# Two cross-product layers on one core: whole first loads, one weight transfer, one sum moved to VectorE and a few copies moved on ScalarE

## The chip, the cores and the metric

The kernel runs on one core of a Trainium2 chip. The metric is the device time of one execution in microseconds. The kernel before took 2045.71 us (median of four runs, 2044.89 to 2046.76). Five engines matter: TensorE (PE; its weight loads are shown apart as PEld), VectorE (DVE), ScalarE (ACT), GpSimd (POOL) and SyncE (SP), which issues most of the DMAs.

## The reference

The input `r_x` has 4096 rows, 32 fields and 16 values per field. Everything runs in float32. A layer multiplies every channel of its input with every field of `x`, mixes the products with a weight matrix and normalises over rows and values:

```python
def _cin_layer(out, x, W, b, gamma, beta):
    r, _, e = x.shape
    h = jnp.einsum('rne,rfe->rnfe', out, x).reshape(r, -1, e)
    h = jnp.einsum('rce,oc->roe', h, W) + b[None, :, None]
    return _batchnorm(h, gamma, beta)
h1 = _cin_layer(x, x, W1, b1, g1, beta1)
out, direct1 = (h1[:, :64], h1[:, 64:])
direct2 = _cin_layer(out, x, W2, b2, g2, beta2)
agg = jnp.concatenate([direct1, direct2], axis=1)
return agg.sum(axis=-1)
```

The batch norm needs the mean and the variance over all rows before the second layer can begin, so the kernel has two stages with a short passage between them.

## The kernel before, in words

The 65536 sites (rows times values) are cut into 128 tiles of T = 512 sites.

**Stage one** walks over the tiles t = 0 to 127. As x times x is symmetric, each tile needs 512 + 16 products and not 1024. `load_main(t)` fetches two tiles, `a` and `b` (128 partitions by 1024 floats, 512 KB each, on SP's queue). VectorE multiplies them into `z` (line 387, 128x2048), and four matmuls with `w1_sb[:, 0..3]` add it up in a bank `ps` (line 428). The 16 products that are left of each tile are computed for eight tiles at once in `zr` (line 373, from `r`), and four small matmuls with `w1_sb[:, 4..5]` add them for four tiles (line 380). ScalarE then evicts the bank three times (lines 352, 355, 358), VectorE takes the statistics (line 115) and a sum (line 364). Tiles rotate through pools: `lpool` has 4 buffers, `zpool` 4, `psum` 6 banks. The weights are the sum of two halves of W1: ScalarE's queue loads `w1_sb` (line 308) and `w1m_sb` (line 309), 384 KB each, and POOL adds them in four pieces (line 312).

The beginning is special. Three matmuls of ones (line 239, "begun") occupy TensorE while the first data are on the way. Tile 0's `a` and `b` are loaded in halves of 256 KB (line 294), in the order a, b, b, a, and the products of tiles 0 and 1 are made in 128x512 pieces (line 396). For tiles 0 and 1 the leftovers come last on TensorE, after the eight matmuls. In this part of the program a scheduler sets the order of each engine's instructions from its own model of time; an edit can therefore move instructions that it doesn't touch.

**The passage**: the last four tiles are computed in halves so that the kept 64 channels come first (line 461). Their statistics give the scale `keep`, and the direct channels are multiplied while the second stage's first products are being made.

**Stage two** walks over 64 pairs of tiles c and, in each, over four stages k (the groups i of 16 kept channels, in the order 3, 0, 1, 2). It uses a Strassen-like scheme with seven products in place of eight. The order in which it issues its work is written out by hand: `queue` chains each engine's instructions. Per stage (c, k):

- ScalarE makes two factors, `f1` and `f2`, by normalising the kept channels into PSUM (line 659, `f<-a,keep`; two buffers, shared with `b11`, ScalarE's PSUM copy of one block of `zz`).
- VectorE multiplies them with `b` and `bx` into `zz` (line 667, two of 128x2048 per stage; stage (0, 0) in four pieces, line 672).
- T2 has two halves. `sum_first` lets POOL make the first (line 703, 128x512), `sum_rest` lets VectorE make the second (line 662, `t<-zz,b`), and POOL then makes T1 and T4 (line 714, 128x2048; in the first stages in two pieces of 128x1024). Stage (0, 0) needs no T.
- TensorE (line 698) runs x2, then the previous stage's `x54` (which needs T1 and T4), then `x31`, then `x67`, 28 passes in all. A pair's sums lie in four banks: X2 and X1, X6 and X2, X3 and X4, X5 and X7. With six banks for two pairs, the next pair's X3/X4 bank is the one that held X1; its first writer is `x31` in stage k = 0.
- `combine(c - 1)` runs in steps (`next(steps)`) among the stages of pair c. Its first step is three ScalarE copies out of the X1 bank (`both`, `both`, `e`); it comes in stage k = 0 after `f1` of the next stage has been queued. VectorE adds (`both`, `u`, `e`, `e`) and a reduction (line 833) follow. In k = 3 of the first seven pairs VectorE takes one more piece of postponed work from `idle` (line 641, statistics; line 364; line 137).

Of the kernel before, what the change touches and what calls it, by code (L numbers as in the profile page):

```python
# [41 lines left out]
FP = mybir.dt.float32  # L42
AF = mybir.ActivationFunctionType
ALU = mybir.AluOpType
AX = mybir.AxisListType

P = 128
ROWS, FIELDS, EMB = 4096, 32, 16
SITES = ROWS * EMB
HALF = SITES // 2  # L50
T = 512
# [5 lines left out]
WRAP = 48  # L57
# [10 lines left out]


@with_exitstack  # L70
def tile_cin(ctx: ExitStack, tc: tile.TileContext, xa, xb, xr, w1, w1m, w2, bn, out):
    nc = tc.nc

    const = ctx.enter_context(tc.tile_pool(name="const", bufs=1))
# [10 lines left out]
    def load_bn():  # L85
        bn_sb = const.tile([P, 6], FP, tag="bn", name="bn_sb")
        nc.scalar.dma_start(bn_sb, bn)
        return bn_sb
# [6 lines left out]
    class Stats:  # L95
# [15 lines left out]
        def add(self, h):  # L111

            if self.at == 0:
                self.stats = spool.tile([P, SG, 6], FP, tag=f"stats{self.name}", name=f"stats{self.name}")
            nc.vector.bn_stats(self.stats[:, self.at, :], h)  # L115
            self.at += 1
            if self.at == self.sizes[self.group]:
                group = self.groups[:, self.group]
                nc.vector.bn_aggr(group[:, 1:3], self.stats[:, : self.at].rearrange("p a b -> p (a b)"))
                nc.vector.tensor_scalar(group[:, 2:3], group[:, 2:3], float(self.at * T), None, ALU.mult)  # L120
                self.at = 0
                self.group += 1
# [83 lines left out]
    for g in range(NC // DIFF):  # L206
        at = 14 + 24 * g
# [7 lines left out]
    loads = []  # L215
# [12 lines left out]
    def queue(engine, make):  # L228

        with tc.issue_after(lasts[engine].ins) if engine in lasts else nullcontext():  # L230
            lasts[engine] = make()
        return lasts[engine]
# [5 lines left out]
    for _ in range(BEGIN):  # L238
# [7 lines left out]
        out=select,  # L246
# [16 lines left out]
    with ExitStack() as one:  # L263
# [5 lines left out]
        zpool = one.enter_context(tc.tile_pool(name="zpool", bufs=4))  # L269
# [5 lines left out]
        def load_rem(g):  # L275

            r = rpool.tile([P, 2 * T], FP, tag="r", name="r")
            with tc.issue_after(loads[-1].ins) if loads else nullcontext():
                nc.sync.dma_start(r, bass.AP(xr.tensor, xr.offset + g * P * 2 * T, [[2 * T, P], [1, 2 * T]]))
            return r  # L280

        def load_main(t):
            a = lpool.tile([P, 2 * T], FP, tag="a", name="a")
            b = lpool.tile([P, 2 * T], FP, tag="b", name="b")

            def load(to, part, n):
                at = part * T
                if to is a:
                    at += xa.offset + t * FIELDS * 2 * T
                    source = bass.AP(xa.tensor, at, [[2 * T, FIELDS], [0, 4], [1, n * T]])  # L290
                else:
                    at += xb.offset + (t * WRAP + 2) * T
                    source = bass.AP(xb.tensor, at, [[T, FIELDS], [4 * T, 4], [1, n * T]])
                return nc.sync.dma_start(to[:, part * T : (part + n) * T], source)

            if t == 0:

                parts = ((a, 0, 1), (b, 0, 1), (b, 1, 1), (a, 1, 1))
            else:
                parts = ((a, 0, 2), (b, 0, 2))  # L300
            for part in parts:
                last = load(*part)
            loads.append(last)
            return a, b

        w1_sb = wpool.tile([P, 6, P], FP, tag="w1", name="w1_sb")
        w1m_sb = zpool.tile([P, 6, P], FP, tag="z", name="w1m_sb")
        nc.scalar.dma_start(w1_sb, w1)
        nc.scalar.dma_start(w1m_sb, w1m)

        for k in (slice(0, 1), slice(1, 2), slice(2, 4), slice(4, 6)):
            nc.gpsimd.tensor_tensor(w1_sb[:, k], w1_sb[:, k], w1m_sb[:, k], ALU.add)  # L312
        bn_sb = load_bn()
        w2_sb = const.tile([P, 16, P], FP, tag="w2", name="w2_sb")
        s_sb = const.tile([P, 4, 4, 2, KEEP], FP, tag="s", name="s_sb")
        neg_sb = const.tile([P, 2, 2, KEEP], FP, tag="neg", name="neg_sb")
# [80 lines left out]

        ending = NT - ENDING
        main = [load_main(t) for t in range(FIRST)]
        r = load_rem(0)  # L400
        for t in range(NT - ENDING):
            s = t % GROUP
# [6 lines left out]
            z = zpool.tile([P, 2, 2, T], FP, tag="z", name="z")  # L409
# [84 lines left out]
        for c in range(NC - ENDING // 2, NC):  # L494
# [3 lines left out]
            for half, k in enumerate(ks):  # L498
                at = half_of[half]
                to = h[:, half * T : (half + 1) * T]  # L500
# [28 lines left out]
        for c in range(NC - ENDING // 2, NC):  # L529
# [10 lines left out]
            for half, k in enumerate(ks):  # L540
                at = half_of[1 - half]
                bias = (b1, b1_swapped)[half][at]
                to = eds[c][half_of[half]]
# [120 lines left out]
    def multiply(z, a, b):  # L664

        a = a.unsqueeze(1).unsqueeze(1).to_broadcast([P, 2, 2, T])
        dve(lambda: nc.vector.tensor_tensor(z, a, b.rearrange("p (k q) t -> p k q t", k=2), ALU.mult))  # L667

    def multiply_part(z, a, b, q):

        a = a.unsqueeze(1).to_broadcast([P, 2, T])
        dve(lambda: nc.vector.tensor_tensor(z[:, :, q], a, b.rearrange("p (k q) t -> p k q t", k=2)[:, :, q], ALU.mult))

    def factor(a, i, half):
        f = factors.tile([P, T], FP, tag="f", name="f")
        act(f, a[:, half * T : (half + 1) * T], scale=keep[:, i, 0:1], bias=keep[:, i, 1:2])
        return f
# [19 lines left out]
            self.started.add(x)  # L697
            queue("pe", lambda: nc.tensor.matmul(self.of[x], w, b, start=start, stop=stop))  # L698

    def sum_first(z):  # L700

        t2 = tpool.tile([P, 2, T], FP, tag="t2", name="t2")
        queue("pool", lambda: nc.gpsimd.tensor_tensor(t2[:, 0], z[:, 1, 0], z[:, 0, 0], ALU.add))  # L703
        return t2

    def sum_rest(z, b11, t2, by_q, by_k):

        t14 = upool.tile([P, 2, 2, T], FP, tag="t14", name="t14")
        add(t2[:, 1], z[:, 1, 1], b11)
        twice = t2.unsqueeze(1).to_broadcast([P, 2, 2, T])  # L710
        parts = (slice(0, 1), slice(1, 2)), (slice(0, 2),)
        for k in parts[not by_k]:
            for q in parts[not by_q]:
                queue("pool", lambda: nc.gpsimd.tensor_tensor(t14[:, k, q], z[:, 2 + k.start : 2 + k.stop, q], twice[:, k, q], ALU.subtract))  # L714
        return t2, t14
# [132 lines left out]
    steps, steps_before = iter(()), iter(())  # L848
# [7 lines left out]
    for c in range(NC):  # L856
        raw, b, bx = following
        sums_ = Sums()

        for k, i in enumerate(STAGES):  # L860

            z = z2pool.tile([P, 4, 2, T], FP, tag="zz", name="zz")
            t = None
            if c == k == 0:

                for q in range(2):
                    multiply_part(z[:, 0::3], f1, b, q)
                    multiply_part(z[:, 1:3], f2, bx, q)
            else:
                multiply(z[:, 0::3], f1, b)  # L870
                if k == 1:

                    next(steps, None)
                f2 = factor(raw[i], i, 1)
                b11 = factors.tile([P, T], FP, tag="f", name="b11")
                act(b11, z[:, 0, 1])
                if k == 1:

                    next(steps, None)
                multiply(z[:, 1:3], f2, bx)  # L880
                t2 = sum_first(z)

            next(steps_before if k == 0 else steps, None)
            if k == 3 and idle:
                dve(idle.pop(0))
            if c > 0 or k > 0:
                t = sum_rest(z, b11, t2, (c, k) <= (1, 0), (c, k) == (NC - 1, 3))
            if k < 3:
                f1 = factor(raw[STAGES[k + 1]], STAGES[k + 1], 0)
            elif c + 1 < NC:  # L890
                following = loaded(c + 1)
                f1 = factor(following[0][STAGES[0]], STAGES[0], 0)

            next(steps, None)
            for _ in range(min(len(sums_left), 4 if c == NC - 1 else 1)):
                queue("act", sums_left.pop(0))
            stage = Stage(sums_, i, z, t, k == 3)
            if c == k == 0:
                stage.ordinary()
            elif (c, k) == (NC - 1, 3):  # L900
                stage.at_last(waiting)
            else:
                stage.x2()
                if waiting:
                    waiting.x54()
                stage.x31()
                stage.x67()
            if c > 0 or k > 0:
                waiting = stage

            if c == 9 and k == 2:
                queue("act", direct_factors)
            if 10 <= c < 14 and k == 2:
                queue("act", lambda: scale_direct(c - 10))
            if c == 15 and k == 2:
                with tc.issue_after(loads[-1].ins):
                    write_direct()
        steps, steps_before = combine(c, sums_), steps
# [12 lines left out]
    part = ROWS // 8  # L931
# [77 lines left out]
```

## Time and profile before

| | |
|---|---|
| four runs | 2046.76, 2044.89, 2046.28, 2045.14 us (median 2045.71) |
| the profiled execution | 2046.76 us, its span 2045.0 us |
| stage one | from 8.85 us (first matmul on data) to about 480 |
| passage | about 480 to 492 us |
| stage two | 492 to 2028 us on TensorE |
| tail after TensorE's last matmul | about 17 us of the span |
| busy share | PE 99%, DVE 96%, POOL 73%, ACT 58% |
| one 128x512 pass of a matmul | 0.43 us apart in stage one, half of that on the mean in stage two (two halves of the array run side by side) |
| first seven transfers to land | w1 3.8, a 5.5, w1m 6.5, b 7.4, the second halves 8.0 and 8.6, tile 1's a 9.9 us |

All times within the execution are counted from the start of its span. A line of the timeline gives the start, the duration, the engine, the source line, the operation, what it writes and reads, the shapes, and in brackets how long the engine was idle before it and what ended that. "SPq" and "ACTq" are the issues of DMAs on these queues. A line of the view by stretches gives the stretch, its length, the busy time of each engine with its number of instructions, then the granted TensorE clock as a share of full speed, the share of the DMA engines' time and the rate. In the table of waits the columns are the total, the count and the longest.

### The profile page before, as it was taken

The numbers are of one execution on the slowest core, as the hardware profiler recorded it, in microseconds if no ns is written. First come the engines' busy times: TensorE is split into PE (matmuls) and PEld (weight loads), VectorE is DVE, ScalarE is ACT, GpSimd is POOL, SyncE is SP. The second block draws the span as 40 slices with busy tenths as digits, with TensorE's granted clock in tenths as the row PEclk, the third lists the DMA queues.
The fourth block names the chain that finished last, engine by engine and source line by source line (L and its number), as shares of the span: only waits on it lengthen the run. The fifth ranks groups of instructions, "written<-read, shape, count | busy, mean of one in ns | idle before, by whom it ended". The sixth has DMA issues, their size and how long they took to land.

```text
span 2045.0 us, 24467 instructions
## 1 busy us (share of the span) xinstructions
PE 2028.2 (99%) x8500; PEld 870.6 (43%) x8500; DVE 1960.7 (96%) x1521; ACT 1185.6 (58%) x1914; POOL 1483.8 (73%) x525
## 2 busy tenths in 40 slices
PE   9999999999999999999999999999999999999997
PEld 3444444443344444444444444444444444444443
DVE  8998988988999999999999999999999999999997
ACT  4555555554566666565666555656665565566564
POOL 0000000002999999999999999999999999999996
PEclk9999999999999999999999999999999999999999
DMA  9999999996777777777776767777767677777661
GB/s 391 371 345 366 352 364 370 371 357 191 177 177 179 178 174 173 196 173 184 180 175 166 175 171 179 176 178 182 175 165 175 172 174 184 179 177 175 167 163 42
DMA packets 112380, 440.70 MB, mean 215 GB/s; under 512 B 13056, under 2 KB 13056, under 8 KB 103808
## 3 DMA queue, kind: packets, MB, share of 16 engines
q1 hardware_dynamic: 105840, 418.43, 73.0%
q10 hardware_dynamic: 6416, 20.72, 2.6%
q8 instruction: 66, 1.08, 0.2%
q14 instruction: 58, 0.48, 0.1%
HBM read 417.07 MB, written 22.02 MB: 215 GB/s over the span
## 4 chain that ended last, share of the span: by engine, by line
PE 98%; DVE 1%; issue 0%; POOL 0%; DMA 0%; ACT 0%; DVEq 0%; ACTq 0%; POOLq 0%
PE x L698 74%; PE ps L428 21%; PE ps L380 2%; PE ps L461 1%; DMA w1m_sb<-in_w1m 0%; POOL t L714 0%; DVE zz L667 0%; DVE d L934 0%; POOL w_sb L312 0%; ACT u L659 0%; DVE both L662 0%; ACT both L659 0%; POOL t L703 0%; DVE d L833 0%; DVE t L662 0%
## 5 line engine op out<-in xcount | busy, mean ns | idle before, releaser
L714 POOL TENSOR_TENSOR t<-zz,t 128x2048 f32<-128x2048 f32 (+1 forms) x260 | 1161.7, 4469 | 20.7 <-DVE t L662 0.9
L698 PE MATMUL x<-t,s_sb 128*64 128x512 f32 x2040 | 958.3, 592 | 0.4 <-POOL t L714 0.4
L698 PE MATMUL x<-zz,s_sb 128*64 128x512 f32 x2048 | 933.7, 592 | 0.0
L698 PE MATMUL x<-zz,w_sb 128*64 128x512 f32 x2056 | 759.1, 592 | 0.0
L703 POOL TENSOR_TENSOR t<-zz 128x512 f32<-128x512 f32 x255 | 326.5, 1280 | 521.0 <-DVE zz L667 520.4
L667 DVE TENSOR_TENSOR zz<-f,bx 128x2048 f32<-128x2048 f32 x255 | 582.2, 2283 | 19.4 <-ACT f L659 19.4
L659 ACT ACTIVATE f<-a,keep 128x512 f32<-128x512 f32 x512 | 398.2, 778 | 342.8 <-DVE zz L667 296.4
L667 DVE TENSOR_TENSOR zz<-f,b 128x2048 f32<-128x2048 f32 x255 | 582.4, 2284 | 0.1
L698 PEld LDWEIGHTS x<-t,s_sb 128*64 128x64 f32 x2040 | 279.2, 137 | 495.5 <-issue 467.2
L698 PE MATMUL x<-t,w_sb 128*64 128x512 f32 x1020 | 479.3, 592 | 0.0
L428 PE MATMUL ps<-z,w_sb 128*128 128x512 f32 x992 | 435.9, 597 | 2.3 <-POOL w_sb L312 2.3
L698 PEld LDWEIGHTS x<-zz,s_sb 128*64 128x64 f32 x2048 | 279.5, 137 | 251.7 <-issue 244.9
L387 DVE TENSOR_TENSOR z<-a,b 128x2048 f32<-128x2048 f32 (+1 forms) x127 | 288.5, 2273 | 42.0 <-PE ps L428 33.1
L428 PEld LDWEIGHTS ps<-z,w_sb 128*128 128x128 f32 x992 | 186.4, 190 | 250.0 <-issue 237.5
L698 PEld LDWEIGHTS x<-zz,w_sb 128*64 128x64 f32 x2056 | 236.7, 137 | 123.6 <-issue 121.5
L659 ACT ACTIVATE b<-zz 128x512 f32<-128x512 f32 x255 | 152.3, 597 | 187.3 <-DVE zz L667 187.3
L352 ACT ACTIVATE e<-ps,bn_sb 128x512 f32<-128x512 f32 x124 | 85.2, 687 | 221.1 <-PE ps L428 201.3
L662 DVE TENSOR_TENSOR t<-zz,b 128x512 f32<-128x512 f32 x255 | 173.3, 680 | 0.4
L698 PEld LDWEIGHTS x<-t,w_sb 128*64 128x64 f32 x1020 | 139.6, 137 | 0.0
L596 ACT ACTIVATE unread<-e,center 128x512 bf16<-128x512 f32 x122 | 86.2, 706 | 0.0
L358 ACT ACTIVATE ed<-ps,bn_sb 64x512 f32<-64x512 f32 x124 | 84.8, 684 | 2.3
L115 DVE BATCH_NORM_STATS2 stats<-e 128x6 f32<-128x512 f32 x124 | 85.1, 687 | 1.1 <-ACT e L352 1.1
(103 smaller groups left out, 866.4 us busy)
## 6 DMA issues: line engine op xcount, KB each, us to landing
a<-h SPq DMA_DIRECT2D x256, 512.0 KB, 4.5
b<-in_xb SPq DMA_DIRECT2D x64, 1024.0 KB, 8.4
a<-in_xa SPq DMA_DIRECT2D x127, 512.0 KB, 6.6
b<-in_xb SPq DMA_DIRECT2D x127, 512.0 KB, 7.7
bx<-in_xb SPq DMA_DIRECT2D x64, 512.0 KB, 8.4
bx<-x SPq DMA_DIRECT2D x64, 512.0 KB, 10.2
h<-kept ACTq DMA_DIRECT2D x64, 256.0 KB, 5.6
r<-in_xr SPq DMA_DIRECT2D x16, 512.0 KB, 9.0
```

The lines of the kernel that those rows point to most:

```text
L115: nc.vector.bn_stats(self.stats[:, self.at, :], h)
L352: nc.scalar.activation(e, ps, AF.Identity, bias=b1)
L358: done = nc.scalar.activation(ed[to, :], ps[KEEP:, :], AF.Identity, bias=b1[KEEP:])
L387: return nc.vector.tensor_tensor(z[:, k], a.rearrange("p (a t) -> p a t", a=2)[:, k].unsqueeze(2).to_broadcast([P, n, 2, T]), b.rearrange( ...
L428: nc.tensor.matmul(pss[t], w1_sb[:, m, :], z[:, m // 2, m % 2, :], start=t < FIRST and m == 0, stop=t >= FIRST and m == 3,)
L596: return nc.scalar.activation(unread, e[:, s], AF.Square, bias=center[:, s], accum_out=squares[:, s, c : c + 1])
L659: return queue("act", lambda: nc.scalar.activation(to, source, AF.Identity, **scale_bias))
L662: return dve(lambda: nc.vector.tensor_tensor(to, x, y, ALU.add))
L667: dve(lambda: nc.vector.tensor_tensor(z, a, b.rearrange("p (k q) t -> p k q t", k=2), ALU.mult))
L698: queue("pe", lambda: nc.tensor.matmul(self.of[x], w, b, start=start, stop=stop))
L703: queue("pool", lambda: nc.gpsimd.tensor_tensor(t2[:, 0], z[:, 1, 0], z[:, 0, 0], ALU.add))
L714: queue("pool", lambda: nc.gpsimd.tensor_tensor(t14[:, k, q], z[:, 2 + k.start : 2 + k.stop, q], twice[:, k, q], ALU.subtract))
```

## The change

There are three parts.

1. The beginning. Every `load_main` issues two whole loads of 512 KB, tile 0 included (four transfers of 256 KB before). The host packs the main weights (pieces 0 to 3) of both halves side by side: one transfer `w1_both` of 512 KB on ScalarE's queue, with 4 KB in each row, in place of two of 384 KB. VectorE adds them in one 128x512 instruction (line 298 of the changed kernel), placed ahead of the products. Pieces 4 and 5 of both halves (`left_both`, 256 KB) are loaded on SP's queue behind the loads of tiles 0 and 1 and ahead of `r`, and POOL adds them (128x256).
2. In stage (0, 1) of stage two, VectorE makes both halves of T2. POOL's line 703 is left out there.
3. In the pairs c = 1 to 4, the three copies out of the X1 bank are queued on ScalarE ahead of `f1` of stage (c, 1), and no longer behind it. (Pair 0 has no pair before it to combine.)

The order of the built program shows three more movements. SP issues two DMAs fewer ahead of tile 1's loads and one more (`left_both`) ahead of `r`. In stage one VectorE's order is changed over the first 20 tiles: the first `BNStats` stands ahead of tile 3's product, where it stood behind it, and later ones move by one or two places. TensorE's order is the same throughout.

```diff
@@ tile_cin: load_main and the weights
-            def load(to, part, n):
-                at = part * T
-                if to is a:
-                    at += xa.offset + t * FIELDS * 2 * T
-                    source = bass.AP(xa.tensor, at, [[2 * T, FIELDS], [0, 4], [1, n * T]])
-                else:
-                    at += xb.offset + (t * WRAP + 2) * T
-                    source = bass.AP(xb.tensor, at, [[T, FIELDS], [4 * T, 4], [1, n * T]])
-                return nc.sync.dma_start(to[:, part * T : (part + n) * T], source)
-
-            if t == 0:
-
-                parts = ((a, 0, 1), (b, 0, 1), (b, 1, 1), (a, 1, 1))
-            else:
-                parts = ((a, 0, 2), (b, 0, 2))
-            for part in parts:
-                last = load(*part)
-            loads.append(last)
+            nc.sync.dma_start(
+                a, bass.AP(xa.tensor, xa.offset + t * FIELDS * 2 * T, [[2 * T, FIELDS], [0, 4], [1, 2 * T]])
+            )
+            at_b = bass.AP(xb.tensor, xb.offset + (t * WRAP + 2) * T, [[T, FIELDS], [4 * T, 4], [1, 2 * T]])
+            loads.append(nc.sync.dma_start(b, at_b))
             return a, b
...
-        w1m_sb = zpool.tile([P, 6, P], FP, tag="z", name="w1m_sb")
-        nc.scalar.dma_start(w1_sb, w1)
-        nc.scalar.dma_start(w1m_sb, w1m)
-
-        for k in (slice(0, 1), slice(1, 2), slice(2, 4), slice(4, 6)):
-            nc.gpsimd.tensor_tensor(w1_sb[:, k], w1_sb[:, k], w1m_sb[:, k], ALU.add)
+        w1_both = zpool.tile([P, 2, 4, P], FP, tag="z", name="w1_both")
+        nc.scalar.dma_start(w1_both, w1)
         bn_sb = load_bn()
+        left_both = zpool.tile([P, 2, 2, P], FP, tag="z", name="left_both")
+        nc.vector.tensor_tensor(w1_sb[:, :4], w1_both[:, 0], w1_both[:, 1], ALU.add)
...
         main = [load_main(t) for t in range(FIRST)]
+
+        nc.sync.dma_start(left_both, w1_left)
+        nc.gpsimd.tensor_tensor(w1_sb[:, 4:], left_both[:, 0], left_both[:, 1], ALU.add)
         r = load_rem(0)
@@ sum_first
-    def sum_first(z):
+    def sum_first(z, at_once):
 
         t2 = tpool.tile([P, 2, T], FP, tag="t2", name="t2")
-        queue("pool", lambda: nc.gpsimd.tensor_tensor(t2[:, 0], z[:, 1, 0], z[:, 0, 0], ALU.add))
+        if at_once:
+            add(t2[:, 0], z[:, 1, 0], z[:, 0, 0])
+        else:
+            queue("pool", lambda: nc.gpsimd.tensor_tensor(t2[:, 0], z[:, 1, 0], z[:, 0, 0], ALU.add))
         return t2
@@ the loop over stages
-                t2 = sum_first(z)
+                t2 = sum_first(z, (c, k) == (0, 1))
...
                 t = sum_rest(z, b11, t2, (c, k) <= (1, 0), (c, k) == (NC - 1, 3))
+            if k == 0 and c < 5:
+
+                next(steps, None)
             if k < 3:
                 f1 = factor(raw[STAGES[k + 1]], STAGES[k + 1], 0)
...
-            next(steps, None)
+            if k > 0 or c >= 5:
+                next(steps, None)
@@ kernel: the host packs the weights
+    w1_both = np.stack([w1t, w1m], axis=1)
...
-    for name, a in (("xa", xa), ("xb", xb), ("xr", xr), ("w1", w1t), ("w1m", w1m), ("w2", w2t), ("bn", bn)):
+    for name, a in (("xa", xa), ("xb", xb), ("xr", xr), ("w1", w1_both[:, :, :4]), ("left", w1_both[:, :, 4:]), ("w2", w2t), ("bn", bn)):
```

More of the change, by code (lines that the diff above doesn't have):

```diff
@@ L70, in tile_cin @@
 @with_exitstack
-def tile_cin(ctx: ExitStack, tc: tile.TileContext, xa, xb, xr, w1, w1m, w2, bn, out):
+def tile_cin(ctx: ExitStack, tc: tile.TileContext, xa, xb, xr, w1, w1_left, w2, bn, out):
     nc = tc.nc
```

## The prediction

> **What bounds the kernel now.** I read the page first, then the table of TensorE's waits, then the beginning by stretches and by the timeline, and last stage two engine by engine.
>
> ```profile
> PE 2028.2 (99%) x8500; PEld 870.6 (43%) x8500; DVE 1960.7 (96%) x1521; ACT 1185.6 (58%) x1914; POOL 1483.8 (73%) x525
> PE 98%; DVE 1%; issue 0%; POOL 0%; DMA 0%; ACT 0%; DVEq 0%; ACTq 0%; POOLq 0%
> ```
>
> TensorE is the bound, and the change takes none of its work away. All it can win is time in which TensorE waits or runs slowly.
>
> ```profile
> PE ps L428 <- POOL w_sb L312: 2.3, 1, 2.3
> PE begun L239 <- DVE ones L236: 1.6, 1, 1.6
> PE x L698 <- POOL t L714: 0.4, 1, 0.4
> ```
>
> These are all of TensorE's waits: 4.3 us. The 1.6 stays. The 2.3 us is the gap between the ones and the first data. Its label is not the last cause: the products are.
>
> ```profile
> 7.49 1.26 DVE L396 TENSOR_TENSOR z<-a,b 128x512 f32<-128x512 f32 x1 [5.86 <-DMA b<-in_xb]
> 8.85 0.77 PE L428 MATMUL ps<-z,w_sb 128*128 128x512 f32 x1 [2.33 <-POOL w_sb L312]
> 6.66 2.67 POOL L312 TENSOR_TENSOR w_sb<-w_sb,w1m_sb 128x128 f32<-128x128 f32 x4 [4.17 <-DMA w1m_sb<-in_w1m]
> 9.80 1.28 DVE L396 TENSOR_TENSOR z<-a,b 128x512 f32<-128x512 f32 x2
> ```
>
> VectorE waits for `b`, begins at 7.49 and ends at 8.75, and TensorE starts 0.10 later. That piece took 1.26 us beside POOL's adds; at 9.80, with POOL done, two took 1.28 (0.6 to 0.7 each).
>
> ```profile
> 7.00:8.00 1.00, 0.00 (x0) 0.00 (x0) 0.51 (x1) 0.39 (x2) 1.00 (x3) 1.00 1.07 420
> 9.00:10.00 1.00, 1.00 (x2) 0.12 (x3) 1.00 (x2) 0.00 (x0) 0.33 (x1) 0.64 1.06 434
> 10.00:11.00 1.00, 1.00 (x2) 0.61 (x2) 1.00 (x2) 0.00 (x0) 0.00 (x0) 0.50 1.00 410
> 11.00:12.00 1.00, 1.00 (x3) 0.35 (x2) 0.88 (x3) 0.00 (x0) 0.00 (x0) 0.50 1.02 418
> 12.00:13.00 1.00, 1.00 (x3) 0.51 (x2) 1.00 (x2) 0.00 (x0) 0.00 (x0) 0.66 1.04 426
> ```
>
> The first share after the counts is the granted clock: 0.64, 0.50, 0.50, 0.66 from 9 to 13 us. The loss is 0.36 + 0.50 + 0.50 + 0.34 = 1.70 us, and it follows the 2.3 us gap. It is as large as the gap itself.
>
> In stage two VectorE is as full as TensorE for the first seven pairs:
>
> ```profile
> 564.00:588.00 24.00, 24.00 (x114) 10.26 (x112) 24.00 (x19) 14.47 (x24) 23.19 (x9) 1.00 0.73 174
> 900.00:924.00 24.00, 24.00 (x114) 10.52 (x112) 22.74 (x17) 15.51 (x28) 22.54 (x8) 1.00 0.66 164
> ```
>
> The third busy time is VectorE's: 24.00 of 24.00 there, 22.74 later. Until 760 us no idle of VectorE is put down to another engine. TensorE leans on it:
>
> ```profile
> 612.20 0.78 ACT L659 ACTIVATE f<-a,keep 128x512 f32<-128x512 f32 x1 [1.60 <-DVE zz L667]
> 614.32 0.59 ACT L659 ACTIVATE e<-x 64x512 f32<-64x512 f32 x1
> 614.96 0.13 PEld L698 LDWEIGHTS x<-zz,s_sb 128*64 128x64 f32 x1 [0.82 <-ACT e L659]
> ```
>
> Pair 5: VectorE's product ends, `f1` follows, then the three copies (the last is `e`), then TensorE's `x31`. Its matmuls stand 0.59 us apart there, where 0.43 is usual. So at 614.96 TensorE is pinned to VectorE's clock.
>
> **The change, part by part.** The sum is made against the profiled execution: 2046.76 us (span 2045.0 and 1.8 around it), 1.05 above the median of the four.
>
> *First data.* Until `b` landed (issue 1.53 plus 5.9, so 7.4) the engines had moved 0.03 + 0.27 + 0.32 + 0.30 + 0.29 + 0.35 + 0.4 x 0.42 = 1.73 MB; w1, w1m, and the halves of a and b make 1.31 of it, 0.42 was other data. Now w1_both, a and b are 1.57 MB, with the same 0.42 beside them 1.99 MB. With 0.30 MB by 3.0 us as before, 1.69 MB at 0.42 a us (the stretches of 4 KB rows) end at 7.0; at the 0.315 of 3 to 7 us, with 0.42 from 7 on, at 8.0. I take 7.3, near the first, since all rows are now of 4 KB. So the larger transfers themselves win 0.1 (from -0.4 to +0.6).
>
> *First product.* POOL adds nothing then, so the piece takes 0.68, not 1.26: -0.58. VectorE's add of the weights (a 128x512 piece, 0.68) waits for w1_both; w1 with 384 KB landed at 3.8, w1m at 6.5, so it ends by 4.5 to 7.2, inside VectorE's 5.86 us of idleness; past 7.3 it would cost its 0.68, since the products stand behind it. TensorE starts at 7.3 + 0.08 + 0.68 + 0.10 = 8.16 in place of 8.85: **-0.69** (7.9 to 8.9: -1.0 to +0.05).
>
> *The clock.* The gap shrinks from 2.33 to 1.65 us. Either the half clock comes anyway (0) or not (-1.70); no run shows a gap of 1.65. The other executions help: 2044.89 and 2045.14 lie 1.9 and 1.6 below the profiled one, about this loss, as if the gap of 2.33 had already escaped it half the time. A shorter gap should escape more often. I take **-1.70**. [...]
>
> *What is late next.* With the full clock the 16 passes of tiles 0 and 1 end at 8.16 + 16 x 0.43 = 15.1, the leftovers (1.07) at 16.2. Tile 2's first product was ready at 16.25 before; it is not later, as the bytes ahead of it are the same (`left_both` is what w1 lost): nothing, at most 0.1. Tile 3's product began at 17.49; now the first `BNStats` stands ahead of it (0.60 by pitch), so it ends near 20.1 less up to 0.4 for earlier landings, while TensorE wants it at 16.2 + 3.5 = 19.7: **+0.4** (0 to 0.6), and 0 at half clock (TensorE wants it at 21.5). Behind that product VectorE's others queue, but tile 4 is wanted only after another 3.5 + 1.07 us.
>
> *`left_both` and POOL.* Its add (0.72 to 1.17 before) falls beside tile 1's pieces and may stretch two of them to 1.2: these end by 13.6 plus 1.2, `zr` included, against 15.1: nothing. SP issues one DMA fewer ahead of tile 2's loads, and the DMA engines were full anyway. [...]
>
> *T2 on VectorE.* Before: POOL 498.84 to 500.12, VectorE's half 498.81, next product 499.56. Now VectorE adds at 498.81 and 499.41, and the product starts at 500.01: +0.45 for VectorE. POOL can start T1 at 499.5 instead of 500.20, but its next job waits for VectorE's product of (0, 2), ending 0.45 later at 504.5, where POOL started it at 504.84: it gains some 0.2 of the 0.7. TensorE's one stall in stage two (0.4 in the table, 0.63 by starts at 528.86) shrinks by that 0.2, but TensorE meets VectorE again in pair 5, so this saves nothing.
>
> *The copies.* In pair 1, ScalarE is free at 513.85 (`b11`, 0.45 later), and `x31` of (0, 3) ends about then. Three copies at a pitch of 0.61, 0.71 and 0.55 put `f1` at 515.8, where VectorE's product alone would have let it start at 515.45: VectorE loses another 0.33. In pairs 2 to 4 the reduction (1.13) and T2 (0.60) stand between, longer than the 0.3 or so left over: 0. The copies end 2 us earlier there, but TensorE did not stall on them in those pairs.
>
> VectorE thus runs 0.45 + 0.33 = 0.78 late, and having no idle time it is still so in pair 5, where the copies come after `f1` as before: **+0.78** on TensorE. Bounds: -0.63, the whole stall won and nothing lost; +2.3, all three copies (1.88) ahead of `f1`. I take 0.78, as the saturated rows from 516 on leave no cover.
>
> Sum: 2046.76 - 0.69 - 1.70 + 0.40 + 0.78 = **2045.5 us**, 0.2 below the median: no change. A measurement tells 0.2% (4.1 us) from nothing.
>
> **The rivals.**
> - *Half clock anyway.* The gap is still there, and 2.33 us did it. 2046.76 - 0.69 + 0.78 = 2046.9.
> - *Stage two keeps its gain.* If `f1` is not late and VectorE regains its 0.45 in small idles (0.1 each at 498, 504 and 515), TensorE wins 0.2 to 0.6 there: 2046.76 - 0.69 - 1.70 + 0.40 - 0.40 = 2044.4. Against it: the pair-5 row.
> - *Whole loads bring nothing.* `b` lands at 8.0, TensorE starts at 8.86 and falls to half clock: 2046.76 + 0.78 = 2047.5. For it: 20% more bytes are needed first, and the early stretches ran at 0.3 MB a us.
> - *Slower by over 0.2%: copies block ScalarE.* They must wait for TensorE's `x31` of the last stage. If ScalarE stood w before them in each of four pairs, VectorE would lose 1.88 + w - 1.73 in pairs 2 to 4 and more in pair 1; from w = 0.9 on this passes 4.1 us, to about 2050. Against it: in pair 1 w is under 0.1.
>
> **How the numbers follow.** Forecast 0.45; half clock 0.20; gain kept 0.20; loads late 0.12; blocking 0.03. The range 2044.3 to 2047.0 leaves out the last two. Faster by over 0.2% needs 2041.6, past every bound here: 0.01. Slower: blocking, 0.03. Within: 0.96.
>
> **What would show it.** Right: the first data matmul near 8.2, `b` at 7.3, a first piece of 0.68, a granted clock of 1.00 from 9 to 13 us, a stall of some tenths at tile 3; in stage two `f1` of pair 1 about 0.8 later after `zz` than before, and pair 5's `x31` waiting longer for `e`. Wrong: a clock of 0.50 after the gap; TensorE's stage two no longer than before; `b` later than 7.6.

## The result and the profile after

The changed kernel takes 2048.64 us (median of 41 runs, 2048.18 to 2051.63); the kernel before took 2046.13 us (median of 61, 2044.70 to 2049.07). By the medians it is 2.5 us slower. That is under the 4.1 us of the 0.2% bound, as forecast, but 1.6 us above the top of the range and on the other side of before. The ratio is 1.0015, with a 95% interval of 1.0011 to 1.0020 (that of the two means is 1.0015 too, that of the medians 1.0012). The profiled execution took 2050.87 us, its span 2049.1.

Both kernels' times lie in two groups, since some executions meet the half clock at the beginning and some do not (shown below). Of before, 26 of 61 lie at 2044.7 to 2045.8 (median 2045.1) and the other 35 at 2046.0 to 2049.1 (2046.7); of the changed kernel, 28 of 41 lie at 2048.2 to 2049.2 (median 2048.5) and 13 at 2050.2 to 2051.6 (2050.5). The mean granted clock of each execution goes with the groups: of the 33 executions of before taken alongside the first four experiments, 13 of the 14 in the lower group have 0.998 and all 19 in the upper one 0.997. At the same clock the loss is thus 3.4 to 3.8 us.

The page of the changed kernel, first the busy times, then the chain that ended last:

```profile
PE 2031.2 (99%) x8500; PEld 888.0 (43%) x8500; DVE 1961.2 (96%) x1523; ACT 1186.3 (58%) x1914; POOL 1489.1 (73%) x521
PE 94%; DVE 2%; POOL 2%; issue 1%; ACT 1%; DMA 1%; DVEq 0%; SPq 0%; ACTq 0%; POOLq 0%
```

The chain leaves TensorE for 6% of the span; before it was 2%. That is where the chain runs, and no measure of the loss: 4% would be 82 us. TensorE's own waits in the changed kernel:

```profile
PE ps L416 <- DVE z L381: 2.2, 1, 2.2
PE begun L239 <- DVE ones L236: 1.6, 1, 1.6
PE x L686 <- DVE both L650: 1.2, 2, 0.9
```

They sum to 5.0 us (4.3 before). This table hides most of the loss: the passes of stage two stand 0.43 us apart and each is shown 0.59 us long, so one that starts 0.16 us late still touches the one before it, and a stall that the starts put at 0.63 us (at 528.86 in the kernel before) is 0.4 in the table. The distance between landmarks does not hide it. From TensorE's first matmul of stage two to its weight load for `x31` in pair 7 it took 171.10 us before and 174.90 now; from there to TensorE's end 1369.31 in both. (That end is at 2032.6 us before and 2036.5 now, with some 12.5 us of the span behind it in both; the 2028 us in the table ahead is TensorE's busy time.) **The 3.8 us lie in the first seven pairs.** To the start of stage two the two profiled executions differ by 0.15 us (492.15 and 492.30).

The beginning of the changed kernel in the timeline:

```profile
7.91 0.69 DVE L381 TENSOR_TENSOR z<-a,b 128x512 f32<-128x512 f32 x1 [2.60 <-DMA b<-in_xb]
8.66 0.70 PE L416 MATMUL ps<-z,w_sb 128*128 128x512 f32 x1 [2.17 <-DVE z L381]
19.30 0.69 DVE L115 BATCH_NORM_STATS2 stats<-e 128x6 f32<-128x512 f32 x1 [2.09 <-ACT e L337]
```

The first product takes 0.69 us (1.26 before), but `b` landed at 7.81, so TensorE begins only 0.19 us earlier, after a gap of 2.17 us. The `BNStats` that now stands ahead of tile 3's product lets VectorE wait 2.09 us for the eviction of tile 0; TensorE lost 0.2 us at tile 3. The clock, in the view by stretches:

```profile
9.00:10.00 1.00, 1.00 (x2) 0.29 (x1) 1.00 (x3) 0.00 (x0) 0.00 (x0) 0.61 1.00 381
10.00:11.00 1.00, 1.00 (x3) 0.48 (x2) 0.99 (x2) 0.00 (x0) 0.00 (x0) 0.50 1.04 420
12.00:13.00 1.00, 1.00 (x2) 0.28 (x2) 1.00 (x2) 0.00 (x0) 0.30 (x1) 0.69 1.04 426
```

In this execution the granted clock fell to one half as before. In stage two VectorE, which had been full, now is not:

```profile
540.00:564.00 24.00, 23.06 (x107) 9.90 (x105) 23.13 (x19) 13.77 (x23) 21.50 (x9) 1.00 0.59 146
564.00:588.00 24.00, 23.70 (x110) 11.44 (x108) 23.07 (x18) 14.05 (x23) 21.95 (x9) 1.00 0.68 169
```

VectorE's busy time (the third) is 23.1 in both, where it was 24.0, and in the next stretch, 588 to 612 us, 22.97 for 23.90: 0.9 us lost in each. The timeline of pair 2 shows how, first ScalarE, then VectorE:

```profile
539.76 0.69 ACT L647 ACTIVATE both<-x,b_swapped 64x512 f32<-64x512 f32 x1
541.85 0.59 ACT L647 ACTIVATE e<-x 64x512 f32<-64x512 f32 x1 [1.40 <-DVE d L824]
542.47 0.78 ACT L647 ACTIVATE f<-a,keep 128x512 f32<-128x512 f32 x1
...
540.61 1.21 DVE L824 TENSOR_REDUCE d<-e 128x64 f32<-128x1024 f32 x1
541.73 0.68 DVE L650 TENSOR_TENSOR t<-zz,b 128x512 f32<-128x512 f32 x1
543.28 2.29 DVE L655 TENSOR_TENSOR zz<-f,b 128x2048 f32<-128x2048 f32 x1 [0.87 <-ACT f L647]
```

The second copy ends at 540.45. The third, into `e`, does not start before 541.85, for 1.40 us, until VectorE's reduction of the *previous* pair's `e` ends at 541.82: `e` has one buffer. Behind the copy stands `f1` (542.47 to 543.25), and behind `f1` VectorE's product, 0.87 us after VectorE was free. Then the lateness reaches TensorE, at a bank that VectorE's `both` add must release, and it is still there in pair 7. The last line is that of before: TensorE waits 0.75 us there in both, but 3.94 us later in the changed kernel, 0.15 of which it had at the start of stage two.

```profile
546.22 0.64 PE L686 MATMUL x<-zz,s_sb 128*64 128x512 f32 x1 [0.94 <-DVE both L650]
667.19 0.13 PEld L686 LDWEIGHTS x<-zz,s_sb 128*64 128x64 f32 x1 [0.75 <-ACT e L647]
663.25 0.13 PEld L698 LDWEIGHTS x<-zz,s_sb 128*64 128x64 f32 x1 [0.75 <-ACT e L659]
```

Before, the reduction stood behind the same product of VectorE, but `f1` stood ahead of the copies, so nobody waited behind the third one. Pair 2 of before, ScalarE and then VectorE:

```profile
539.78 0.78 ACT L659 ACTIVATE f<-a,keep 128x512 f32<-128x512 f32 x1 [1.60 <-DVE zz L667]
541.90 0.59 ACT L659 ACTIVATE e<-x 64x512 f32<-64x512 f32 x1
...
539.66 1.21 DVE L833 TENSOR_REDUCE d<-e 128x64 f32<-128x1024 f32 x1
541.38 2.28 DVE L667 TENSOR_TENSOR zz<-f,b 128x2048 f32<-128x2048 f32 x1
```

`f1` is ready at 540.56, the reduction ends at 540.87, the copy into `e` comes only at 541.90, and VectorE's product at 541.38 waits for nobody.

### The profile page after: what moved, and what is told of

It reads as the page before. It is cut to its first block, busy times and chain, and to the rows that moved or that the text cites. A ratio compares the mean times of both kernels' runs of the same rounds, so it can differ in the third digit from the quotient of the medians.

```text
span 2049.1 us, 24459 instructions
## 1 busy us (share of the span) xinstructions
PE 2031.2 (99%) x8500; PEld 888.0 (43%) x8500; DVE 1961.2 (96%) x1523; ACT 1186.3 (58%) x1914; POOL 1489.1 (73%) x521
## 4 chain that ended last, share of the span: by engine, by line
PE 94%; DVE 2%; POOL 2%; issue 1%; ACT 1%; DMA 1%; DVEq 0%; SPq 0%; ACTq 0%; POOLq 0%
PE x L686 71%; PE ps L416 21%; PE ps L365 2%; POOL t L705 1%; DVE zz L655 1%; PE ps L449 1%; POOL t L694 0%; DMA b<-in_xb 0%; ACT f L647 0%; DVE d L824 0%; DMA a<-h 0%; DVE zz L660 0%; DVE both L650 0%; ACT e L647 0%; DVE z L372 0%
```

## The experiments

The measure of stage two below is the landmark distance (171.10 us before). "VectorE idle" is VectorE's waiting for `f1` from the end of stage (0, 0) up to 760 us, in the table of waits: the total and, in brackets, how many waits.

| kernel | stage two, us | VectorE idle | median, us | ratio to before |
|---|---|---|---|---|
| before | 171.10 | none | 2046.13 | |
| changed | 174.90 | 3.2 (4) | 2048.64 | 1.0015 (1.0011 to 1.0020) |
| part 3 alone | 174.87 | 3.6 (4) | 2050.30 | 1.0018 (1.0010 to 1.0027) |
| part 2 alone | 171.46 | none | 2046.87 | 1.0004 (0.9995 to 1.0013) |
| part 1 alone | 171.08 | none | 2044.60 | 0.9997 (0.9989 to 1.0006) |
| part 3, two buffers of e | 171.87 | 0.9 (1) | 2047.18 | 1.0008 (0.9999 to 1.0017) |
| changed, two buffers of e | 171.89 | 0.5 (1) | 2046.27 | 1.0004 (0.9995 to 1.0013) |
| part 3 in pair 1 only | 171.89 | 0.9 (1) | 2047.24 | 1.0005 (0.9996 to 1.0014) |
| two of three copies ahead | 171.29 | 0.3 (1) | 2045.36 | 1.0004 (0.9995 to 1.0012) |
| parts 1 and 2 | 171.47 | none | 2045.52 | 1.0001 (0.9992 to 1.0010) |
| before, five matmuls of ones | 171.08 | none | 2045.25 | 0.9997 (0.9989 to 1.0006) |
| part 1, five of ones | 171.10 | none | 2045.20 | 0.9996 (0.9987 to 1.0005) |
| part 1, four of ones | 171.10 | none | 2045.00 | 0.9998 (0.9989 to 1.0007) |

Medians of eleven runs move by a microsecond with the share of half-clock executions among them; the landmark distance does not, and repeats to 0.02 us between kernels whose stage two is the same.

**Part 3 alone.**

```diff
+            if k == 0 and c < 5:
+                next(steps, None)
             if k < 3:
                 f1 = factor(raw[STAGES[k + 1]], STAGES[k + 1], 0)
...
-            next(steps, None)
+            if k > 0 or c >= 5:
+                next(steps, None)
```

> The kernel before with part 3 alone: in pairs 1 to 4 the three copies stand ahead of f1. In the trace of the changed kernel VectorE stands idle for 0.48, 0.87, 0.93 and 0.93 us in these four pairs, 3.2 us in all, where it had no idle before, and TensorE later meets VectorE in pair 5. Theory (the copies are the loss): 2.7 to 3.4 us slower than before, VectorE idle at the same four places. Rival (the second VectorE add of part 2 makes VectorE late, and the copies only show it): at most 1 us slower, and no idle above 0.3 us in pairs 2 to 4.

Stage two takes 174.87 us, 3.77 more than before, all of the changed kernel's loss. VectorE's waits in this kernel (total, count, longest):

```profile
DVE zz L667 <- ACT f L659: 3.6, 4, 0.9
```

0.87, 0.87, 0.93 and 0.93 us in pairs 1 to 4. The loss belongs to part 3; the rival falls. It is somewhat above the 2.7 to 3.4 expected; pair 1 loses 0.87 here and only 0.48 in the changed kernel.

**Part 2 alone.** The `at_once` of `sum_first`, for stage (0, 1), and nothing else.

> The kernel before with part 2 alone: VectorE makes both halves of T2 in stage (0, 1). In the changed kernel's trace the product after it began at 500.10 where it was 499.56, with a stage that began 0.08 later: 0.46 us lost by VectorE. Theory: VectorE has no idle time up to pair 6, so TensorE is later by 0.4 to 0.5 us at pair 5, and the time is 0.3 to 0.6 us above before. Rival: TensorE's stall of 0.63 us in pair 1 goes and nothing is lost: 0.2 to 0.6 us faster.

Stage two takes 0.36 us more (171.46), a little under the 0.4 to 0.5 expected. The saved POOL instruction wins TensorE nothing: its stall in pair 1 gives way to two others (0.2 and 0.6 us, in pairs 1 and 2, where `x31` waits). The time itself is not told from before. The changed kernel's lines show VectorE's 0.46 us; the start of the product was 499.56 before, in a stage that began 0.08 later here:

```profile
498.89 0.69 DVE L650 TENSOR_TENSOR t<-zz 128x512 f32<-128x512 f32 x1
499.50 0.68 DVE L650 TENSOR_TENSOR t<-zz,b 128x512 f32<-128x512 f32 x1
500.10 2.28 DVE L655 TENSOR_TENSOR zz<-f,b 128x2048 f32<-128x2048 f32 x1
```

On top of part 3 it costs nothing (174.90 against 174.87): a VectorE that is 0.46 us later waits 0.39 less for `f1` in pair 1 (0.48 for 0.87).

**Part 1 alone.** The diff's first part and the host's packing.

> The kernel before with part 1 alone: whole first loads and one transfer of the main weights. In the changed kernel's trace b landed at 7.8 us (7.4 before), the first matmul on data came at 8.66 (8.85 before) and the clock fell to one half all the same; at tile 3 TensorE lost 0.2 us behind the first BNStats; at 475 us it was 0.15 us late. Theory: within 0.5 us of before when both meet the half clock; the gap before the first data is 2.2 in place of 2.3 us, so the half clock is met a little less often. Rival (the beginning is a real part of the loss): 1 us slower or more.

Nine of eleven executions lie at 2044.4 to 2044.9, 0.5 us below those of before at full clock (2045.1); two lie at 2046.8 and 2048.6. Stage two is unchanged (171.08). In its profile `b` landed at 7.33, and the gap was 1.16 us:

```profile
8.18 0.70 PE L416 MATMUL ps<-z,w_sb 128*128 128x512 f32 x1 [1.16 <-DVE z L381]
```

```profile
10.00:11.00 1.00, 1.00 (x4) 0.52 (x3) 1.00 (x2) 0.00 (x0) 0.45 (x1) 1.00 1.02 416
```

The second line is from its view by stretches: the clock stays at 1.00. Of the three parts it is the only one whose executions lie mostly below those of before, but the interval of its ratio holds 1, and the kernels with part 1 further down do not all repeat the 0.5 us.

**Part 3 with a second buffer for `e`.**

```diff
+    esums = ctx.enter_context(tc.tile_pool(name="esums", bufs=2))
...
-        e = cpool.tile([P, 2, T], FP, tag="e", name="e")
+        e = esums.tile([P, 2, T], FP, tag="e", name="e")
```

> Part 3 alone as in copies_alone, with two buffers for the tile e of the combination in place of one. Theory A (in pairs 2 to 4 the third copy writes e, whose only buffer is still to be read by the reduction of the pair before; that reduction stands behind VectorE's second product, and f1 stands behind the copy): the idle of 0.9 us goes in pairs 2 to 4, that of 0.5 us in pair 1 stays, and the time is 0.3 to 0.6 us above before. Theory B (the three copies are long, 1.9 us, and push f1 back by themselves, or wait for TensorE): the idle stays, and the time is 2.7 to 3.4 us above before.

The idle of pairs 2 to 4 is gone, that of pair 1 stays, and stage two falls from 174.87 to 171.87 us. That is 0.77 more than before, above the 0.3 to 0.6 that was expected of the time. VectorE's waits, then ScalarE and VectorE in pair 2:

```profile
DVE zz L668 <- ACT f L660: 0.9, 1, 0.9
```

```profile
538.93 0.68 ACT L660 ACTIVATE both<-x,b_swapped 64x512 f32<-64x512 f32 x1
539.63 0.59 ACT L660 ACTIVATE e<-x 64x512 f32<-64x512 f32 x1
540.24 0.78 ACT L660 ACTIVATE f<-a,keep 128x512 f32<-128x512 f32 x1
...
540.91 0.68 DVE L663 TENSOR_TENSOR t<-zz,b 128x512 f32<-128x512 f32 x1
541.50 2.28 DVE L668 TENSOR_TENSOR zz<-f,b 128x2048 f32<-128x2048 f32 x1
```

The third copy now follows the second at once, `f1` is ready at 541.02, and the product starts at 541.50 as soon as VectorE has done T2. Theory A holds, B falls.

**The changed kernel with a second buffer for `e`.** The same edit in the changed kernel.

> The changed kernel with two buffers for the tile e. In part 3 alone the second buffer took VectorE's idle of 0.9 us out of pairs 2 to 4 and left 0.87 in pair 1. Theory (one buffer of e is the whole difference between the forecast and the result in stage two): VectorE idle in pair 1 alone, some 0.5 us; TensorE's way from its last small matmuls of stage one at about 475 us to its short stall in pair 7 takes 188.7 us, 0.8 more than before and 3.0 less than in the changed kernel; time 2045 to 2046, near the forecast of 2045.5. Rival: parts 2 and 3 together hold something else, and more than 1.5 us of the loss stays.

Stage two takes 171.89 us, 0.79 more than before. VectorE's waits:

```profile
DVE zz L656 <- ACT f L648: 0.5, 1, 0.5
```

The forecast had 0.78 us for this stage: with two buffers the sum comes out as forecast. The median, 2046.27, is 0.3 above the range expected: five of the eleven executions lie at 2045.2 to 2045.6, two at 2046.3 to 2046.4 and four above 2047.8. The profiled one (2046.37) had the full clock and a span of 2043.6: 2.8 us lie outside its span, where 1.7 to 1.8 is usual.

**Part 3 in pair 1 only.** `c < 5` becomes `c == 1`.

> The kernel before with the copies ahead of f1 in pair 1 alone, where no reduction of an earlier pair exists and the copies wait for nothing but TensorE and their own length. Theory: VectorE idle once, 0.87 us as in part 3 alone, and TensorE 0.8 us later in pair 7: 0.5 to 1.0 us above before at the same clock. Rival (the loss of part 3 grows from pair to pair, each late pair making the next later): less than 0.3 us here.

One idle of 0.87 us, and 0.79 us on stage two. Pair 1 has no reduction before it; there the copies' own length pushes `f1` back (in the changed kernel's pair 1 `b11` ends at 513.94, the three copies run from 514.07 to 515.96 and `f1` starts at 515.99). The other 3.0 us of part 3 come from pairs 2 to 4.

**Two of three copies ahead.** One buffer, but the step is cut between the copies into `both` and the one into `e`.

```diff
         act(both[high], x21[high], bias=b2_swapped[high])
+        if c < 4:
+            yield
```

The loop has the first hunk of part 3, and its later `next(steps)` stays as it was.

> The kernel before with only the first two copies (both, both) ahead of f1 in pairs 1 to 4; the third (e) stays behind f1. One buffer for e as before. Theory (f1 waits behind the third copy, which waits for the reduction): no idle of VectorE in pairs 2 to 4, about 0.25 us in pair 1 (0.87 less the third copy's 0.6); 0.1 to 0.4 us above before. Rival (any copy ahead of f1 costs VectorE time): 0.3 us or more of idle in each of the four pairs, 1 us above before.

The only idle is 0.27 us in pair 1, and stage two takes 171.29, 0.19 more than before. So in pairs 2 to 4 it is neither copies ahead of `f1` as such nor the wait for TensorE, but the one copy with a reader to wait for.

**Parts 1 and 2 together.** The changed kernel without part 3.

> The changed kernel without part 3: parts 1 and 2 together. Part 1 alone was 0.5 us below before at the same clock, part 2 alone cost 0.35 in the trace. Theory (the parts add up): 2044.7 to 2045.3 for the executions at full clock, 0.1 to 0.3 below before's at full clock; VectorE without idle in pairs 1 to 4. Rival (parts 1 and 2 spoil each other): above 2046 at full clock.

Eight of eleven executions lie at 2044.9 to 2045.6, a little above the 2044.7 to 2045.3 expected. Stage two is 171.47, as with part 2 alone, without any idle of VectorE, and the profiled execution (2045.23) is 0.39 above that of part 1 alone (2044.84): so far the parts add up. Against before they do not: the executions of before taken alongside lie around 2045.1 at full clock, these eight around 2045.5, where -0.5 and +0.36 would make -0.1. So the 0.5 us of part 1 is not seen here, and why is open.

**Before with five matmuls of ones.** `BEGIN = 5`.

> The kernel before with five matmuls of ones at the beginning in place of three. They run until about 7 to 8.2 us, so the gap before the first data shrinks from 2.3 to between 0.6 and 1.8 us; the first data come no earlier. Theory (the gap decides whether the clock falls to one half for 3.4 us, which costs 1.7): no time is near 2046.7 any more, all lie near 2045.0, and the granted clock is 1.00 from 9 to 13 us. [...]

All eleven executions lie at 2044.88 to 2045.63; 33 of before, taken alongside, ran from 2044.84 to 2047.89, and 19 of them lie in the upper group. So the gap makes that group. In its profile `b` landed as late as 7.75, and the data still met a full clock:

```profile
10.00:11.00 1.00, 0.96 (x2) 0.17 (x3) 1.00 (x2) 0.00 (x0) 0.31 (x1) 1.00 1.03 422
```

**Part 1 with five, and with four.**

> Part 1 alone with five matmuls of ones. Part 1 alone had nine of eleven executions at 2044.4 to 2044.9 and two above 2046.8. Theory: the gap is now under 1.5 us and all executions lie at 2044.4 to 2044.9: 0.4 to 0.6 us below the better executions of before, 1.2 to 1.6 us below its median; the faster start is then cut by the 0.2 us that TensorE loses at tile 3. Rival: the ones run into the first data, and the time is 0.3 us or more above part 1 alone.

> Part 1 alone with four matmuls of ones. With three, two of eleven executions met the half clock; with five, the ones ran until 8.6 us into the first data that were ready at 7.9. With four they end by 7.4 us at the latest, ahead of the first product (7.9 to 8.6). Theory: all executions between 2044.4 and 2045.0, 1.2 to 1.5 us below the median of before, and the lowest median of all kernels here. Rival (a late b still leaves a gap that meets the half clock): one or more in eleven above 2046.

With five, the first data's matmul came at 9.03, though `b` had landed at 7.11: the ones were in the way, and the times spread from 2044.45 to 2046.82, where 2044.4 to 2044.9 was expected; its median is 0.6 above that of part 1 alone, as the rival had it (the two were not taken alongside each other). With four, all eleven executions lie at 2044.45 to 2045.41, five of them above the 2045.0 expected. Its median in the table is 1.1 us under the median of before over 61 runs, but that of before taken alongside was 2045.18, the interval of the ratio holds 1, and part 1 alone (three) has a lower median with two executions above 2046. None of its executions lies in the upper group, as with five in the kernel before; that it beats before by more than some tenths is not shown.

**The gap and the clock over all profiles.** The gap is TensorE's wait for the first data, the clock the mean over 8 to 14 us.

| gap, us | 0, 0, 0.3 | 1.1, 1.2, 1.4 | 1.7, 1.8 | 2.2, 2.3, 2.4, 2.9 | 3.0 |
|---|---|---|---|---|---|
| mean clock | 1.00 | 1.00 | 1.00 | 0.72 | 0.50 |

In 13 profiles there is no exception, but between 1.8 and 2.2 us nothing was measured. What ends the gap varies: `b` landed between 7.14 and 8.00 us in seven profiles with halves (median 7.41), between 6.97 and 7.81 in six with whole loads (median 7.25). What begins it varies more: the passes of the ones stand 0.85 us apart at first and 0.43 later, the change comes at another pass in each execution, and three matmuls of ones ended between 5.78 and 7.04 us. The gap of part 1 alone is 1.17 us shorter than that of before; the earlier data make 0.67 of it, and 0.50 is the end of the ones, 7.02 for 6.52, which the change doesn't touch.

## Why the prediction was wrong

- **The bound, and where to look**: right. TensorE's work is unchanged, the loss is waiting, and it reaches TensorE through a VectorE that has no slack up to pair 7 (before, no wait of it for another engine from 492 to 760 us).
- **The copies, "in pairs 2 to 4 ... longer than the 0.3 or so left over: 0"**: this step failed. It took the three copies as free to run once `b11` and `x31` were done. The third one writes `e`, whose one buffer is read last by the reduction, and the working itself put that reduction behind VectorE's second product, as cover. It was the cover and the obstacle at once: 0.87, 0.93 and 0.93 us. In pair 1, which has no reduction, the term was 0.33 forecast and 0.48 measured.
- **The rival "copies block ScalarE"** had the place and the form right and the wrong thing waited for. It priced a wait w for TensorE's `x31`, found it under 0.1 in pair 1 and gave the case 0.03. In pair 2 ScalarE stood 1.40 us, for VectorE. Its price was too high, since wait and cover overlap: 0.9 us a pair and not 1.88 + 1.40 - 1.73.
- **T2 on VectorE, +0.45**: VectorE lost 0.46, TensorE 0.36 alone; on top of the copies it costs nothing. That POOL's gain saves nothing: right.
- **The whole of stage two, +0.78**: 3.80 measured; 0.79 with the second buffer, where the step's assumption holds. That this meets the forecast to 0.01 is in part luck: the two pieces show on VectorE as 0.46 and 0.48, 0.94 together, and part 3 in pair 1 alone costs TensorE the same 0.79 without the T2 add.
- **First data**: the product's 0.68 was 0.69. `b` at 7.3 was 7.81 in this execution, inside the bounds of 7.0 to 8.0, and 6.97 to 7.33 in five other profiles with whole loads. The rate from 4 to 7 us, forecast at 0.42 MB a us for rows of 4 KB, was 0.36 to 0.39 here, and 0.41 to 0.42 in the changed kernel with two buffers of `e`, where `b` landed at 6.97. The gain in the start was 0.19 for the 0.69 forecast.
- **The clock, -1.70**: wrong for the profiled execution, where `b` came late and the gap was 2.17. That a gap of 1.65 escapes is borne out by the profiles with 1.7 and 1.8. What the working left out is that the ones end at another moment in each execution (three of them between 5.78 and 7.04 us): it held their end fixed, and took the two faster executions of before for a gap of 2.33 that had escaped, while the gap itself varies (1.1 to 3.0 us in the ten profiles with three matmuls of ones). Over all executions the upper group shrank from 35 of 61 to 13 of 41. A gap of 2.17 us was followed by the half clock and one of 1.78 was not; between them nothing was measured.
- **What is late next, +0.4, and 0 at half clock**: 0.2 in both. At half clock the `BNStats` waits for an eviction that comes late with TensorE (2.09 us in the changed kernel), which the working left out.
- **The sum**: 2045.5 forecast, 2048.64 measured. In the profiled execution the missed 3.0 of stage two, the 1.7 of the clock and the 0.5 by which the first data came later make up most of the 5.4 us between 2045.5 and 2050.87.

A part of TensorE's lateness is not traced: in part 3 alone VectorE's idle times sum to 3.60 us and TensorE loses 3.77.

## What to carry to other kernels

Before an instruction is moved ahead in an engine's queue, list all that it waits for, the last reader of the buffer that it writes above all: everything that now stands behind it inherits that wait (in pair 2 the copy into `e` waited 1.40 us, and VectorE's product, behind `f1`, 0.87), and a piece of work counted as cover may be the very thing waited for. Where an engine is full, measure from landmark to landmark, since a stall hardly shows in busy shares (TensorE's is 99% in both kernels) and only in part in the table of waits (0.7 us more there, 3.8 between the landmarks). A few matmuls of ones that reach up to the first data took away the slower group of the times (five of them in the kernel before, or four with part 1: no execution of eleven above 2045.63), which the faster arrival of these data only made smaller (13 of 41 in the changed kernel, 35 of 61 before); too many stand in the way of the data (five with part 1: the first data's matmul at 9.03, with `b` landed at 7.11).

## What the runs showed of the hardware

In 13 profiles the mean granted clock from 8 to 14 us was 0.50 or 0.72 after every gap of 2.17 us or more at the beginning and 1.00 after every gap of up to 1.78 us (in the profiled executions of before and of the changed kernel it stood at 0.50 from 10 to 12 us). The times of one unchanged kernel lie in two groups 1.6 us apart (2045.1 and 2046.7). The same first transfer of `b` lands up to 0.9 us apart (7.14 to 8.00 us over seven kernels with the same loads), more than part 1 was meant to win, and the same three matmuls of ones end up to 1.3 us apart (5.78 to 7.04).
